# Per-batch quantiser shifts, an earlier set-up of the second pass, and a verdict by a matrix product in a four-block attention kernel

## The chip, the cores and the metric

The kernel runs on one core of a Trainium2 chip. The core has a matrix engine (TensorE, PE), a vector engine (VectorE, DVE), an engine for elementwise functions (ScalarE, ACT), a general engine (GpSimd, POOL) and an engine that only issues transfers (SyncE, SP). Each works through its own instructions in the order in which the program was built, and waits on semaphores for the others. Transfers (DMAs) are issued from SP and from POOL and run beside them. The metric is the device time of one execution in microseconds (us), the median of several.

## The reference

Four attention blocks work one after the other on `x` (4 batches, 1024 tokens, 288 channels, 16 heads of 18). Blocks 0 and 3 have quantised linear layers, block 1 is a plain attention with a second set of keys. The change lies in block 2, whose attention quantises its inputs and its probabilities with one step for the whole tensor, cut from the reference:

```
def _fake_quant(x, n_bits, always_zero=False):
    levels = float(2 ** n_bits - 1)
    if always_zero:
        delta = stop_gradient(jnp.max(x) / levels); zp = 0.0
    ...
    xq = jnp.clip(_ste_round(x / delta) + zp, 0.0, levels)
    return (xq - zp) * delta

q, k, v = (_fake_quant(t, 8) for t in (q, k, v))
probs = jax.nn.softmax(einsum('bhqd,bhkd->bhqk', q, k) * scale, axis=-1)
probs = _fake_quant(probs, 8, always_zero=True)
out = einsum('bhqk,bhkd->bqhd', probs, v).reshape(b, s, 288) @ Wo + bo
...
h = h + _quant_attention(ln(h), ln(h), Wq1, ...)      # over 1024 tokens
h = h + _quant_attention(ln(h), context, Wq2, ...)    # over 64 context tokens
h = h + (a * gelu(gate)) @ Wff2 + bff2                # a, gate = ln(h) @ Wff1 + bff1
```

The step of the probabilities is the largest probability of the whole tensor, divided by 255. So no probability can be rounded before every row's sum and maximum are known.

## The kernel before

The kernel keeps `x` in on-chip memory and runs blocks 0 to 3. It counts on input ranges in which its short forms hold: the helper `watch_range` (L1213) writes for each watched tensor whether it left its range into a column of `bad`. At the end `verdict` (L1197) joins the columns, and if any is set the program runs a general path instead of keeping its result. A branch on the loaded value stands on every engine.

Block 2 has three stages.

*Stage 1* makes the queries, keys and values and writes them to a scratch area in main memory, with their global minima and maxima.

*`fq_passes`* (L2812) is the attention over 1024 tokens. Pass 1 reads queries, keys and values back (`in<-raw`, issued on SP), rounds them to levels, transposes them on PE, and ACT copies them into `qk` (all batches' queries and keys, head by head). The helper `operands` does a tile's transposes and copy; those of batch b+1 are placed among the scores of batch b. Then, for each batch, group of heads, 128 queries and pair of heads, PE makes scores (L3244), ACT takes two exponentials with row sums (L2891) into a buffer `e`, of which there are four (pool `f1e`), and DVE takes the row maxima `top` (L2898): 256 such steps.

Between the passes `prob_shift` (L2365) computes for each row and head the number that, added to the row's scores, makes the exponential come out directly as a quantiser level: reciprocal of the sums (L2373), range watch, product with `top`, maximum over all (`prob_params`, L820: on DVE, then on POOL by `partition_all_reduce`), then `log_shift` (L830) with a logarithm on ACT (L837) corrected by one exponential (L840), and the result split into three bf16 parts (L2383). All of this works on one 128x512 array, which is 32 tiles of 16 heads. ACT loads a function table between Ln and Exp. `add_shift` (L2389) puts a tile's three parts beside the 18 channels of each head: POOL copies them into `spad` (L2393), PE transposes (L2399), DVE adds to `qk` (L2400). Queries of a group of heads are multiplied with `kz`, a copy of the keys spread over zeros; `kz` is zeroed once by POOL and filled by DMAs on SP (`spread`, L2999; four transfers a turn, two tiles `kz0` and `kz1` in turn).

Pass 2 (`attend_levels`, L3253) makes the scores again (L3284), exponentials (L3293), rounding on DVE (L3296) and products with the values. The shifts of later tiles, the output projection and the next queries are made beside it.

*`fq_tail`* is the attention over 64 context tokens and the feed-forward part. It too calls `prob_shift`, with `top` and `sums` in the pool `f2q`. Behind it SP loads the feed-forward weights (L2408, L113) into memory that this pool has given back, then a bias (L3117) and, for each half batch, the queries (`qT<-qb`, L3127). POOL's copies into `spad` and the rest of `add_shift` follow for each tile.

What sets the order: the framework collects the program, assigns each instruction to its engine and lists them there by a scheduler that moves instructions by the time at which it thinks them ready. So the text's order and an engine's order can differ. Memory comes from pools on a stack: what a new pool takes from one that was closed must wait until the last user of the old one has finished. That wait stands on the engine that first writes the new memory. In the kernel before, the pool `f1o` (with `g2`, `b2`, `bo2`, `wq2`, `spad`, `kz`) is opened after the pool of `top` and `sums` was closed.

Of the kernel before, what the change touches and what calls it, by code (L numbers as in the profile page):

```python
# [18 lines left out]

# [2 lines left out]

# [6 lines left out]
F32 = mybir.dt.float32  # L29
BF16 = mybir.dt.bfloat16  # L30
I32 = mybir.dt.int32
AF = mybir.ActivationFunctionType
ALU = mybir.AluOpType
# [3 lines left out]
P = 128  # L37
B, S, C, H, D, T, FF = 4, 1024, 288, 16, 18, 64, 1152
NTB = S // P
NT = B * NTB  # L40
CK, NC3 = 96, 3
HP = 32
NG = 4
# [1135 lines left out]
class Fast(Net):  # L1179
# [16 lines left out]
    def verdict(self):  # L1196

        nc = self.nc
        s = self.cp.tile([P, 1], F32, name="bads")
        nc.vector.tensor_reduce(s, self.bad, AX.X, ALU.max)  # L1200
        al = self.cp.tile([P, 1], F32, name="bada")
        nc.gpsimd.partition_all_reduce(al, s, P, bass_isa.ReduceOp.max)
        fl = self.cp.tile([1, 1], mybir.dt.int32, name="badi")
        nc.vector.tensor_copy(fl, al[0:1, :])
        return nc.values_load(fl[0:1, 0:1])

    @contextmanager
# [1157 lines left out]
    def prob_shift(self, gp, tp, top, sums, step):  # L2365


        nc = self.nc
        flat = lambda ap: ap.rearrange("p t h -> p (t h)")
        rstep = gp.tile([P, 1], F32, name="rstep")  # L2370
        nc.vector.reciprocal(rstep, step)
        r = tp.tile([P, NT * H], F32, name="rs")
        nc.vector.reciprocal(r, flat(sums))  # L2373
        self.watch_range(self.R_MIN, self.R_MAX, r, "wr")
        u = flat(top)
        nc.vector.tensor_tensor(r, r, u, ALU.mult)
        pd = self.prob_params(gp, r, "pd")
        nc.vector.memset(u, 0.0)
        self.log_shift(tp, u, flat(sums), pd, "ls")
        nc.vector.tensor_scalar(u, u, rstep, None, ALU.mult)  # L2380
        parts = gp.tile([P, 3, NT * H], BF16, name="parts")
        for k in range(3):
            nc.vector.tensor_copy(parts[:, k, :], u)  # L2383
            if k < 2:
                nc.vector.tensor_tensor(u, u, parts[:, k, :], ALU.subtract)
        return pd, parts

    def add_shift(self, qT, sp, parts, t):


        nc = self.nc
        for k in range(3):
            nc.gpsimd.tensor_copy(  # L2393
                sp[:, :, D + k : D + k + 1], parts[:, k, t * H : (t + 1) * H].unsqueeze(2)
            )
        ps = self.ps1(BF16)
        sf = sp.rearrange("p h d -> p (h d)")
        for g in range(NG):
            nc.tensor.transpose(ps[:, g * P : (g + 1) * P], sf[:, g * P : (g + 1) * P], self.idb)  # L2399
        nc.vector.tensor_tensor(  # L2400
            qT, qT, ps[:, : NG * P].rearrange("p (g t) -> p g t", t=P), ALU.add
        )
# [410 lines left out]
    def fq_passes(self, w, q, step, raw, rawq, qmx, qmn, side, aside):  # L2813

        tc, nc = self.tc, self.nc
        with ExitStack() as es:
            pool = lambda name, bufs, **k: es.enter_context(tc.tile_pool(name=name, bufs=bufs, **k))
            gp = pool("f1h", 1)
            wo = gp.tile([P, NG, C], F32, name="wo")
            nc.sync.dma_start(wo, w["Wo1p"].rearrange("(g p) o -> p g o", p=P))  # L2820
            rstep = self.scale_register("lstep", step)
            qk = gp.tile([P, B, 2, NG, S], BF16, name="qk")
            v = gp.tile([P, NT, C + HP - D], BF16, name="v")
            nc.gpsimd.memset(v[:, :, C:], 0.0)

            tops = ExitStack()
            tp = tops.enter_context(tc.tile_pool(name="f1m", bufs=1))
            top = tp.tile([P, NT, H], F32, name="top")
            sums = tp.tile([P, NT, H], F32, name="sums")
            with (  # L2830
                tc.tile_pool(name="f1l", bufs=3) as ld,
                tc.tile_pool(name="f1a", bufs=1) as at,
                tc.tile_pool(name="f1e", bufs=4) as ep,
                tc.tile_pool(name="f1x", bufs=3, space=PSUM) as self.pa,
                tc.tile_pool(name="f1y", bufs=2, space=PSUM) as self.pb,
            ):
# [22 lines left out]
                def operands(b, j):  # L2859

                    ps = self.ps1(BF16)
                    pf = pads[(b * NTB + j) % 4].rearrange("p n h d -> p (n h d)")
                    for m in range(2 * NG):
                        nc.tensor.transpose(
                            ps[:, m * P : (m + 1) * P], pf[:, m * P : (m + 1) * P], self.idb
                        )
                    nc.scalar.copy(
                        qk[:, b, :, :, j * P : (j + 1) * P].rearrange("p n g t -> p (n g) t"),
                        ps.rearrange("p (m t) -> p m t", t=P),
                    )  # L2870
# [3 lines left out]
                for b in range(B):  # L2874
                    ahead = levels(b + 1) if b + 1 < B else None
                    for g in range(NG):
                        for qt in range(NTB):
                            t = b * NTB + qt

                            n = g * NTB + qt  # L2880
# [17 lines left out]
                                nc.vector.tensor_reduce(top[:, t, h0 : h0 + 2], e, AX.X, ALU.max)  # L2898
                    if ahead:
                        operands(b + 1, NTB - 1)  # L2900
            with tops:
                pd, parts = self.prob_shift(gp, tp, top, sums, step)
            es.enter_context(self.psum("f1o"))

            pv = gp.tile([P, 1], F32, name="pv")
            nc.vector.tensor_tensor(pv, pd, q["d"][:, 2:3], ALU.mult)
            nc.vector.tensor_scalar(wo, wo, pv, None, ALU.mult)
            at, ot, ep = pool("f1o", 1), pool("f1q", 2), pool("f1p", 2)
            g2 = self.load_bc(at, w["ln2_g"], C, "g2")
            b2 = self.load_bc(at, w["ln2_b"], C, "b2")  # L2910
            bo2 = self.load_bc(at, w["bo2"], C, "bo2")
            wq2 = self.load_w(at, w["Wq2"], C, "wq2")
            spad = at.tile([P, H, HP], BF16, name="spad")
            nc.gpsimd.memset(spad, 0.0)

            def shifts(b, hf):
                for j in range(hf * 4, hf * 4 + 4):
                    t = b * NTB + j
                    self.add_shift(qk[:, b, 0, :, j * P : (j + 1) * P], spad, parts, t)
                    yield  # L2920

            def output(t0, oT):

                yield
                yield
                for j in range(4):
                    ps = self.ps1()
                    for k in range(NG):
                        nc.tensor.matmul(
                            ps[:, :C],  # L2930
                            lhsT=oT[:, k, j * P : (j + 1) * P],
                            rhs=wo[:, k, :],
                            start=(k == 0),
                            stop=(k == NG - 1),
                        )
                        if k == 1:
                            yield
                    xt = self.x[:, t0 + j, :]
                    nc.vector.tensor_tensor(xt, xt, ps[:, :C], ALU.add)
                    yield  # L2940
# [45 lines left out]
                        nc.sync.dma_start(rawq[t // NTB][:, t % NTB, :], y)  # L2986
                        yield

            kzs = [at.tile([P, 2, S], BF16, name=f"kz{n}") for n in range(2)]
            for kz in kzs:  # L2990
                nc.gpsimd.memset(kz, 0.0)

            def spread(n):

                kz = kzs[n % 2]
                b, g = n // (2 * NG), n % NG
                for i in range(4):
                    rows = slice(i * HP, (i + 1) * HP)
                    nc.sync.dma_start(kz[rows, i % 2, :], qk[rows, b, 1, g, :])  # L2999

            spread(0)
            side.append(shifts(0, 0))
            while side:
                aside()
            late = []
            for b in range(B):
                for qh in range(2):
# [18 lines left out]
    def fq_tail(self, w, kq, keep, rawq, mx, nmn, beside):  # L3026
# [4 lines left out]
        tc, nc = self.tc, self.nc  # L3031
        with ExitStack() as es:
            pool = lambda name, bufs, **k: es.enter_context(tc.tile_pool(name=name, bufs=bufs, **k))
            gp, dr = pool("f2g", 1), pool("f2d", 1, space=bass.MemoryType.DRAM)
            wo = gp.tile([P, NG, C], F32, name="wo")
# [3 lines left out]
            with (  # L3039
# [7 lines left out]
                top = qp.tile([P, NT, H], F32, name="top")  # L3047
                sums = qp.tile([P, NT, H], F32, name="sums")
# [6 lines left out]
                q = self.global_params(gp, mx, nmn, "qq")  # L3055
                self.watch_range(-0.5, 255.5, q["zp"], "qzext")
                step = gp.tile([P, 1], F32, name="step")
# [3 lines left out]
                rstep = self.scale_register("cstep", step)  # L3061

                for t in range(NT):
                    b, j = divmod(t, NTB)
                    pd = pads[t % 3]
# [4 lines left out]
                    ps = self.ps1(BF16)  # L3070
# [9 lines left out]
                    for m in range(2):  # L3080
                        ps = self.ps1()
                        for g in (2 * m, 2 * m + 1):
                            nc.tensor.matmul(
                                ps[:, (g % 2) * 256 : (g % 2 + 1) * 256],
                                lhsT=qT[:, g, :],
                                rhs=kt["kbd4"][:, b, g, :],
                                start=True,
                                stop=True,
# [10 lines left out]
                    e4 = self.wk.tile([P, H, T // 4], F32, tag="e4", name="e4")  # L3099
                    nc.gpsimd.tensor_tensor(e4, e2[:, :, : T // 4], e2[:, :, T // 4 :], ALU.add)  # L3100
                    nc.vector.tensor_reduce(sums[:, t, :], e4, AX.X, ALU.add)
                pd, parts = self.prob_shift(gp, qp, top, sums, step)
            pv = gp.tile([P, 1], F32, name="pv")
            nc.vector.tensor_tensor(pv, pd, kq["d"][:, 1:2], ALU.mult)
            nc.vector.tensor_scalar(wo, wo, pv, None, ALU.mult)
# [302 lines left out]
```

## Time and profile before

| | |
|---|---|
| median of 3 runs | 5169.89 us (5169.68 to 5172.34) |
| the profiled execution, its own time | 5169.41 us |
| its span | 5167.7 us |
| mean granted PE clock | 0.836 |
| busy: PE, ACT, DVE, POOL | 4402.1 (85%), 3131.3 (61%), 2961.2 (57%), 1395.9 (27%) us |
| block 2, pass 1, about | 1854 to 2456 us |
| between the passes, last maximum to first exponential of pass 2 | 2455.84 to 2484.47 us |
| tail: last sum to first exponential after `prob_shift` | 3182.56 to 3220.10 us |
| last `y` done, last residual adds begun, end | 5151.90, 5160.35, 5167.7 us |

The span runs from the first to the last recorded instruction of one execution; the time of that execution is 1.7 us longer. In the views, a group's line has the engine, the operation, the tile written and those read, the shape, then the busy time, the mean duration in ns, and behind the second bar the idle time ahead of it with what ended most of it. A line of the timeline has the start, the duration (of a row of like instructions together, with their number behind x), the engine, and in brackets the idle time before it. "SPq" is an issue of a transfer on SP.

### The profile page before, as it was taken

How to read it: one execution, taken by the hardware profiler on the slowest of the kernel's cores; microseconds unless marked ns; L12 is line 12 of the kernel's file. 1: busy time of each engine (PE TensorE's matmuls, PEld its weight loads, DVE VectorE, ACT ScalarE, POOL GpSimd, SP SyncE). 2: the span in 40 equal slices, each digit the busy share in tenths (PEclk: the TensorE clock that was granted, in tenths of full speed). 3: DMA queues.
4: the chain of work that ended last, by engine and by line, in shares of the span. 5: the costliest groups of instructions: out<-in, count | busy, mean ns of one | idle time of the engine just before them, and what ended most of it. 6: DMA issues, size and time to landing. Idle time of an engine off the chain costs nothing. (4 is left out here: it accounts for less than half of the span.)

```text
span 5167.7 us, 63518 instructions
## 1 busy us (share of the span) xinstructions
PE 4402.1 (85%) x23067; PEld 1767.0 (34%) x23067; DVE 2961.2 (57%) x6478; ACT 3131.3 (61%) x4422; POOL 1395.9 (27%) x2173
## 2 busy tenths in 40 slices
PE   5999997788899979998688863899988999996786
PEld 2223222445566521100232332454542222222343
DVE  8333243665564569999687877432334334334775
ACT  2767665466653259999788853212215766674796
POOL 4020111442421457300122234111113021103664
PEclk8999998889999965555687875899997999997897
DMA  2000002200001221000000032000000000001000
GB/s 74 4 5 12 3 21 54 68 25 15 2 12 40 101 87 35 14 1 0 23 24 24 23 98 79 20 15 10 1 15 1 8 4 9 18 21 31 16 17 20
DMA packets 135541, 135.64 MB, mean 26 GB/s; under 512 B 69260, under 2 KB 111884, under 8 KB 133552
## 3 DMA queue, kind: packets, MB, share of 16 engines
q1 hardware_dynamic: 134016, 127.79, 8.2%
q0 software_dynamic: 1200, 3.69, 0.3%
q8 instruction: 183, 3.00, 0.2%
q14 instruction: 142, 1.16, 0.1%
HBM read 79.59 MB, written 43.47 MB: 24 GB/s over the span
## 5 line engine op out<-in xcount | busy, mean ns | idle before, releaser
L2004 ACT ACTIVATE e<-ps 128x1024 f32<-128x1024 f32 x1024 | 998.9, 1021 | 481.9 <-PE ps L1994 471.3
L1994 PE MATMUL ps<-qT,kT 32*128 32x512 f32 x4096 | 704.4, 662 | 5.2 <-ACT e L2004 5.2
L1954 PE MATMUL ps<-e,v 128*32 128x512 f32 x4096 | 573.6, 625 | 11.4 <-DVE oT L1965 9.1
L2898 DVE TENSOR_REDUCE top<-e 128x2 f32<-128x2048 f32 x256 | 561.9, 2322 | 18.6 <-ACT e L2891 18.6
L2891 ACT ACTIVATE e<-ps 128x1024 f32<-128x1024 f32 x512 | 534.0, 1369 | 19.6 <-PE ps L3244 11.3
L3293 ACT ACTIVATE e<-ps 128x1024 f32<-128x1024 f32 x512 | 484.2, 1056 | 89.7 <-PE ps L3284 71.4
L3244 PE MATMUL ps<-qk 32*128 32x512 bf16 x1024 | 511.1, 604 | 24.3 <-ACT e L2891 23.0
L1747 POOL TENSOR_TENSOR x<-x,y 128x288 f32<-128x288 f32 x192 | 152.0, 803 | 826.3 <-DVE y L1746 758.7
L1404 POOL TENSOR_TENSOR h<-h,g 128x288 f32<-128x288 f32 x224 | 181.5, 813 | 645.5 <-ACT h L1401 606.7
L3296 DVE TENSOR_SCALAR eb<-e 128x2048 bf16<-128x2048 f32 x256 | 321.9, 1261 | 49.3 <-ACT e L3293 47.0
L1994 PEld LDWEIGHTS ps<-qT,kT 32*128 32x128 f32 x4096 | 204.9, 189 | 227.4 <-issue 143.3
L2891 ACT ACTIVATION_READ_ACCUMULATOR e<-ps 128x1 f32 x512 | 280.6, 550 | 0.0
L3284 PE MATMUL ps<-qk,kz 64*128 64x512 bf16 x1024 | 228.9, 445 | 43.0 <-ACT e L3293 39.9
L2437 PE MATMUL psf<-hT,w 128*128 128x512 f32 x576 | 257.9, 600 | 0.6 <-ACT hT L2429 0.6
L1954 PEld LDWEIGHTS ps<-e,v 128*32 128x32 f32 x4096 | 83.0, 109 | 424.4 <-issue 349.5
L1349 PE MATMUL ps<-idb,q 128*128 128x128 bf16 (+2 forms) x1152 | 114.6, 245 | 119.8 <-ACT q L1333 67.7
L1401 ACT ACTIVATE h<-x,nmr,rstd 128x288 f32<-128x288 f32 x224 | 130.2, 622 | 139.2 <-DVE nmr L1393 68.1
L3244 PEld LDWEIGHTS <-qk 32*128 32x128 bf16 x1024 | 52.8, 99 | 465.1 <-issue 465.1
L3193 ACT ACTIVATE gl<-psf,bf 128x512 f32<-128x512 f32 x72 | 46.0, 684 | 270.6 <-PE psf L2441 266.0
L1354 ACT COPY qT<-ps 98x384 bf16<-98x384 bf16 (+3 forms) x256 | 151.6, 641 | 72.6 <-PE ps L1349 72.4
L277 PEld LDWEIGHTS <-qT 98*128 98x128 bf16 (+2 forms) x1344 | 136.1, 105 | 129.9 <-issue 45.5
L1405 POOL TENSOR_TENSOR h<-h,b 128x288 f32<-128x288 f32 x224 | 179.9, 806 | 0.3
(483 smaller groups left out, 7725.3 us busy)
## 6 DMA issues: line engine op xcount, KB each, us to landing
raw<-y SPq DMA_DIRECT2D x32, 432.0 KB
in<-raw SPq DMA_DIRECT2D x32, 432.0 KB
kz<-qk SPq DMA_DIRECT2D x128, 64.0 KB
wn<-in_L_wfc SPq DMA_DIRECT2D x12, 432.0 KB
x<-in_x SPq DMA_DIRECT2D x4, 1152.0 KB
vvo<-vt SPq DMA_DIRECT2D x16, 288.0 KB
vo<-vvo SPq DMA_DIRECT2D x4, 1152.0 KB
rawq<-y SPq DMA_DIRECT2D x32, 144.0 KB
```

The costliest lines, as they stand in the source:

```text
L1404: nc.gpsimd.tensor_tensor(h, h, g, ALU.mult)
L1405: nc.gpsimd.tensor_tensor(h, h, beta, ALU.add)
L1954: nc.tensor.matmul(acc[i * HP : (i + 1) * HP, :], lhsT=st["v"][:, kt, h * (D + 1) : h * (D + 1) + HP], rhs=es_[i // 2][:, i % 2, :], start ...
L1994: nc.tensor.matmul(pss[i // 2][:, i % 2, :], lhsT=self.row_tile(kT, i)[:, kt * P : (kt + 1) * P], rhs=self.row_tile(qT, i)[:, qh * 512 : ( ...
L2004: nc.scalar.activation(e, ps, AF.Exp, scale=SCALE)
L2437: nc.tensor.matmul(o, lhsT=lhs(i)[:, c, :], rhs=rhs(i)[:, c, :], start=(c == 0), stop=False)
L2891: nc.scalar.activation(e[:, j, :].rearrange("p (a n) -> p a n", a=2), sc, AF.Exp, scale=rstep, accum_out=sums[:, t, h0 + j : h0 + j + 1],)
L2898: nc.vector.tensor_reduce(top[:, t, h0 : h0 + 2], e, AX.X, ALU.max)
L3244: self.nc.tensor.matmul(ps[:, c, :], lhsT=self.row_tile(qT, i)[:, g, qt * P : (qt + 1) * P], rhs=self.row_tile(kT, i)[:, g, c * 512 : (c + ...
L3284: nc.tensor.matmul(pss[i][:, n, :], lhsT=kz[rows, i, kt * P : (kt + 1) * P], rhs=qT[rows, g, qh * 512 : (qh + 1) * 512], start=True, stop= ...
L3293: nc.scalar.activation(e[:, 2 * n : 2 * n + 2, :], ps, AF.Exp, scale=step)
L3296: nc.vector.tensor_scalar(eb, e, MAGIC, MAGIC, ALU.add, ALU.subtract)
```

## The change

The change has four parts.

1. `verdict` joins the 128 partitions by a product with a column of ones on PE, in one bank of a new pool, and DVE copies the 1x1 result to an integer. The `partition_all_reduce` on POOL is no longer made.
2. `prob_shift` returns, beside the global step, one function for each batch. Each makes the shift of its 128x128 quarter, with its own tiles `y`, `z` and `parts`. The reciprocal, the product with `top` and the global maximum are still made on the whole. The product goes into `top`, and the range watch moves behind the last batch's shift.
3. `fq_passes` opens the pool `f1o` before the pool of `top` and `sums`, so that the loads, the zeros of `spad` and `kz` and the first keys don't need the memory of `top`. The first `spread` is written right after pass 1. Then come batch 0's shift, its first four tiles, the other batches' shifts, and the scaling of `wo`. The pool of `e` has three buffers instead of four.
4. `fq_tail` calls the four functions one after the other.

```diff
     def verdict(self):
...
-        al = self.cp.tile([P, 1], F32, name="bada")
-        nc.gpsimd.partition_all_reduce(al, s, P, bass_isa.ReduceOp.max)
         fl = self.cp.tile([1, 1], mybir.dt.int32, name="badi")
-        nc.vector.tensor_copy(fl, al[0:1, :])
+        with self.psum8("bad"):
+            ps = self.ps1()
+            nc.tensor.matmul(ps[0:1, 0:1], lhsT=s, rhs=self.ones[:, 0:1], start=True, stop=True)
+            nc.vector.tensor_copy(fl, ps[0:1, 0:1])
         return nc.values_load(fl[0:1, 0:1])
...
     def prob_shift(self, gp, tp, top, sums, step):
...
         nc.vector.reciprocal(r, flat(sums))
-        self.watch_range(self.R_MIN, self.R_MAX, r, "wr")
-        u = flat(top)
-        nc.vector.tensor_tensor(r, r, u, ALU.mult)
-        pd = self.prob_params(gp, r, "pd")
-        nc.vector.memset(u, 0.0)
-        self.log_shift(tp, u, flat(sums), pd, "ls")
-        nc.vector.tensor_scalar(u, u, rstep, None, ALU.mult)
-        parts = gp.tile([P, 3, NT * H], BF16, name="parts")
-        for k in range(3):
-            nc.vector.tensor_copy(parts[:, k, :], u)
-            if k < 2:
-                nc.vector.tensor_tensor(u, u, parts[:, k, :], ALU.subtract)
-        return pd, parts
+        nc.vector.tensor_tensor(flat(top), r, flat(top), ALU.mult)
+        pd = self.prob_params(gp, flat(top), "pd")
+        parts = [gp.tile([P, 3, NTB * H], BF16, name=f"parts{b}") for b in range(B)]
+
+        def shift(b):
+            u = flat(top[:, b * NTB : (b + 1) * NTB, :])
+            nc.vector.memset(u, 0.0)
+            self.log_shift(tp, u, flat(sums[:, b * NTB : (b + 1) * NTB, :]), pd, f"ls{b}")
+            nc.vector.tensor_scalar(u, u, rstep, None, ALU.mult)
+            for k in range(3):
+                nc.vector.tensor_copy(parts[b][:, k, :], u)
+                if k < 2:
+                    nc.vector.tensor_tensor(u, u, parts[b][:, k, :], ALU.subtract)
+            if b == B - 1:
+                self.watch_range(self.R_MIN, self.R_MAX, r, "wr")
+
+        return pd, parts, [partial(shift, b) for b in range(B)]
...
     def add_shift(self, qT, sp, parts, t):
...
-                sp[:, :, D + k : D + k + 1], parts[:, k, t * H : (t + 1) * H].unsqueeze(2)
+                sp[:, :, D + k : D + k + 1],
+                parts[t // NTB][:, k, t % NTB * H : (t % NTB + 1) * H].unsqueeze(2),
...
     def fq_passes(self, w, q, step, raw, rawq, qmx, qmn, side, aside):
...
+            at = pool("f1o", 1)
+            g2 = self.load_bc(at, w["ln2_g"], C, "g2")
+            b2 = self.load_bc(at, w["ln2_b"], C, "b2")
+            bo2 = self.load_bc(at, w["bo2"], C, "bo2")
+            wq2 = self.load_w(at, w["Wq2"], C, "wq2")
+            spad = at.tile([P, H, HP], BF16, name="spad")
+            nc.gpsimd.memset(spad, 0.0)
+            kzs = [at.tile([P, 2, S], BF16, name=f"kz{n}") for n in range(2)]
+            for kz in kzs:
+                nc.gpsimd.memset(kz, 0.0)
+
+            def spread(n):
...
             tops = ExitStack()
...
-                tc.tile_pool(name="f1e", bufs=4) as ep,
+                tc.tile_pool(name="f1e", bufs=3) as ep,
...
-            with tops:
-                pd, parts = self.prob_shift(gp, tp, top, sums, step)
+            spread(0)
+            pd, parts, shift = self.prob_shift(gp, tp, top, sums, step)
             es.enter_context(self.psum("f1o"))
-
-            pv = gp.tile([P, 1], F32, name="pv")
-            nc.vector.tensor_tensor(pv, pd, q["d"][:, 2:3], ALU.mult)
-            nc.vector.tensor_scalar(wo, wo, pv, None, ALU.mult)
-            at, ot, ep = pool("f1o", 1), pool("f1q", 2), pool("f1p", 2)
-            g2 = self.load_bc(at, w["ln2_g"], C, "g2")
...
+            shift[0]()
+            for _ in shifts(0, 0):
+                pass
+            for f in shift[1:]:
+                f()
+            tops.close()
+
+            pv = gp.tile([P, 1], F32, name="pv")
+            nc.vector.tensor_tensor(pv, pd, q["d"][:, 2:3], ALU.mult)
+            nc.vector.tensor_scalar(wo, wo, pv, None, ALU.mult)
+            ot, ep = pool("f1q", 2), pool("f1p", 2)
...
-            kzs = [at.tile([P, 2, S], BF16, name=f"kz{n}") for n in range(2)]
-            for kz in kzs:
-                nc.gpsimd.memset(kz, 0.0)
...
-            spread(0)
-            side.append(shifts(0, 0))
-            while side:
-                aside()
...
     def fq_tail(self, w, kq, keep, rawq, mx, nmn, beside):
...
-                pd, parts = self.prob_shift(gp, qp, top, sums, step)
+                pd, parts, shift = self.prob_shift(gp, qp, top, sums, step)
+                for f in shift:
+                    f()
```

More of the change, by code (lines that the diff above doesn't have):

```diff
@@ L21 @@
 from contextlib import ExitStack, contextmanager
+from functools import partial
 import concourse.bass as bass
@@ L2824, in fq_passes @@
             nc.gpsimd.memset(v[:, :, C:], 0.0)
+            at = pool("f1o", 1)
[9 more added lines that the diff above has]
+            def spread(n):
+                kz = kzs[n % 2]
+                b, g = n // (2 * NG), n % NG
+                for i in range(4):
+                    rows = slice(i * HP, (i + 1) * HP)
+                    nc.sync.dma_start(kz[rows, i % 2, :], qk[rows, b, 1, g, :])
             tops = ExitStack()
@@ L2900, in fq_passes @@
                         operands(b + 1, NTB - 1)
-            with tops:
-                pd, parts = self.prob_shift(gp, tp, top, sums, step)
+            spread(0)
+            pd, parts, shift = self.prob_shift(gp, tp, top, sums, step)
             es.enter_context(self.psum("f1o"))
-            pv = gp.tile([P, 1], F32, name="pv")
-            nc.vector.tensor_tensor(pv, pd, q["d"][:, 2:3], ALU.mult)
-            nc.vector.tensor_scalar(wo, wo, pv, None, ALU.mult)
-            at, ot, ep = pool("f1o", 1), pool("f1q", 2), pool("f1p", 2)
-            g2 = self.load_bc(at, w["ln2_g"], C, "g2")
[L2910 to L2914, printed above, removed]
             def shifts(b, hf):
@@ L2987, in queries @@
                         yield
-            kzs = [at.tile([P, 2, S], BF16, name=f"kz{n}") for n in range(2)]
-            for kz in kzs:
[L2991 to L2999, printed above, removed]
-            spread(0)
-            side.append(shifts(0, 0))
-            while side:
-                aside()
             late = []
```

## The prediction

> **What bounds the kernel now.** I read the page's chain and costliest groups first, then the timeline in four windows: the end, pass 1 of block 2, the hand-over from pass 1 to pass 2, and the start of the tail. The chain that ended last names only the end of the program, so it can't price a change in the middle. The groups give the rate of pass 1.
>
> ```profile
> issue 0%; POOL 0%
> ...
> L2898 DVE TENSOR_REDUCE top<-e 128x2 f32<-128x2048 f32 x256 | 561.9, 2322 | 18.6 <-ACT e L2891 18.6
> L2891 ACT ACTIVATE e<-ps 128x1024 f32<-128x1024 f32 x512 | 534.0, 1369 | 19.6 <-PE ps L3244 11.3
> ```
>
> Pass 1 (1854 to 2456 us) is held by VectorE (DVE): 256 reductions of 2.32 us, with 18.6 us idle in all. ScalarE (ACT) makes one `e` in about 2.0 us against 2.19 us from one reduction's start to the next, so it runs ahead until the buffers of `e` are full.
>
> The hand-over, in the timeline (start, duration, engine, line; in brackets the idle time before and its releaser):
>
> ```profile
> 2455.67 3.43 DVE L2373 RECIPROCAL rs<-sums 128x512 f32<-128x512 f32 x1
> ...
> 2470.60 0.43 DVE L2383 CAST parts<-top 128x512 bf16<-128x512 f32 x1
> ...
> 2471.63 0.74 POOL L107 DMA_DIRECT2D g<-in_L_ln_g  x1 [9.19 <-DVE parts L2383]
> ...
> 2473.90 3.58 POOL L2991 MEMSET kz<- 128x2048 bf16 x2
> ...
> 2477.40 0.54 POOL L2393 COPY spad<-parts 128x16 bf16<-128x16 bf16 x3
> ...
> 2484.47 1.94 ACT L3293 ACTIVATE e<-ps 128x1024 f32<-128x1024 f32 x2 [18.71 <-PE ps L3284]
> ```
>
> One chain: reciprocal, maximum, GpSimd (POOL) all-reduce (2462.07), Ln (2463.19), table load (1.28), Exp (2465.13), ten DVE steps to 2471.03; then POOL's loads and memsets to 2477.48, because the memory they fill is that of `top` and `rs`; then 1.33 us a tile for the shifts, and at 2484.47 the first exponential of pass 2. All engines are in this chain, so a microsecond saved is a microsecond of time.
>
> The tail has the same chain, but its last step releases a queue:
>
> ```profile
> 3197.74 0.49 DVE L2383 CAST parts<-top 128x512 bf16<-128x512 f32 x1
> ...
> 3198.39 0.39 SPq L2408 DMA_DIRECT2D w<-in_L_Wff  x1
> ...
> 3199.35 10.29 SPq L3117 DMA_DIRECT2D bf<-in_L_bff  x1
> ...
> 3217.80 1.52 DVE L2400 TENSOR_TENSOR qT<-qT,ps 128x512 bf16<-128x512 bf16 x4 [19.56 <-DMA qT<-qb]
> ```
>
> SP's weight load needs memory in which `top` stood, so it goes 0.16 us after the last cast; behind it on SP stand the bias load (10.29 us of issue) and the loads of `qT`. DVE is idle 19.56 us for `qT`, ACT 27.27 us. Whatever delays the last cast delays the stage one for one.
>
> The end:
>
> ```profile
> 5151.38 0.52 DVE L1746 SCALAR_TENSOR_TENSOR y<-ps,sc,wfc2sw 128x288 f32<-128x288 f32 x1 [2.61 <-PE ps L277]
> 5152.62 0.38 POOL L1202 PARTITION_ALL_REDUCE bada<-bads  x1 [5.87 <-DVE y L1746]
> 5153.03 0.14 DVE L1204 CAST badi<-bada 1x1 int32<-1x1 f32 x1 [1.13 <-POOL bada L1202]
> 5160.35 1.53 POOL L1747 TENSOR_TENSOR x<-x,y 128x288 f32<-128x288 f32 x2 [7.36 <-issue]
> ```
>
> The all-reduce comes late and, worse, the last two residual adds stand behind it on POOL, 7.36 us with no releaser ("issue"). I read this as POOL changing its program for the all-reduce and back: the trace has records of a new POOL configuration at 5146.9, before it, and at 5152.95, after it. Everything after 5160.35 waits for them.
>
> **What the Trainium skill says.** "ScalarE: Activation LUTs", What ACT_TABLE_LOAD costs: a load is about 1283 ns plus a drain of about 1380 ns. The trace has the load, 1.28 us, but not the drain: Ln ends at 2463.82, Exp starts at 2465.13. Its section on table sets says that one set holds both exp and ln; the trace disagrees for this program, a load stands between them. "VectorE: DVE Perf Modes", on the fixed latency per instruction: an fp32 tensor_tensor takes (N+151)/0.96 ns. For 512 that is 0.69 us, as the trace shows; for 128 it is 0.29 (my estimate from the page), so a quarter of the data costs over 40% of the time. On POOL's program change I found no price; the trace gives 5.87 and 7.36 us.
>
> **The change part by part.**
>
> *Loads, zeros and keys set up ahead.* Three POOL loads, 0.56 us memset, 3.58 us of memsets and one SP load now stand ahead of stage 1's own. POOL idles 44.98 us until 1655.08 (its next load waits for DVE's `bad` of block 1); about 6 us go into this hole, cost nothing. Without that cover they would add 6. The eight key copies (5.04 us of SP issue) go into pass 1 among SP's loads, whose users are many microseconds behind: nothing.
>
> *Three buffers for `e` instead of four.* The program's order also moves the `qk` copies forward: 268 exponentials before the last, instead of 290. An `e` with a copy costs ACT 0.89 us more. Before, DVE's distance behind ACT shrinks through that stretch to 1.04 us at its least, and then grows to 4.3. With three buffers it can hold about one reduction, 2.2 us, and copies now come closer together. Following both engines with those rates I get 0 to 1.9 us of extra idle time on DVE: +1.0. Bounds for the unknown: 0 and +3.
>
> *Shift by batch, hand-over.* One DVE maximum (0.6) leaves the way ahead of the all-reduce (the other still stands there), and other small steps go: all-reduce 0.9 earlier, 2461.15. `Ln` of batch 0 follows at about 2462.1. At 128x128 I take ACT 0.31 (between 0.21 at 128x8 and 0.63 at 128x512), DVE 0.29 for two operands and 0.21 to 0.23 for one, start to start 0.08 less where nothing depends. But ACT's order is now Ln0, Ln1, load, Exp0, load, Ln2, load, Exp1, Exp2, load, Ln3, load, Exp3: six loads instead of two (+4 × 1.28 = 5.1). DVE's in-order stream takes batch 1's product before batch 0's first parts, so three loads stand ahead: Exp1 ends at 2462.1 + 4 × 0.31 + 3 × 1.28 + 0.2 = about 2467.4. Some 14 DVE steps of 0.18: parts of batch 0 at 2469.9 (whole tensor before: 2471.03). POOL's copies then start at once, 0.3 to 0.4 us later the first transpose, 2470.3 against 2477.98. The tiles' cadence stays, so the first exponential comes at 2484.47 − 7.7 = 2476.8; DVE's remaining casts and the scaling of `wo` (0.82) hold back the first `eb` by some 0.2. Gain 7.5, bounds 6 and 8.5. It consists of 6.4 us of POOL work that left the way and 1.1 us of earlier parts.
>
> *Shift by batch, tail.* All four batches are made before anything else, so here the loads and small steps count in full. The maximum comes 0.65 earlier (3188.9). Parts of batch 0 at about 3197.2; batch 3's last DVE product before its Ln stands behind these, so Ln3 3198.1, load, Exp3 to about 3199.9, then some 20 DVE steps of 0.2 (among them `wo`, 0.81): last cast over at 3203.8, against 3198.23. Cost +5.6, bounds +4.5 and +7.5. SP's queue starts by that much later, and `qT` with it.
>
> *Verdict by a product.* No program change: the adds stand directly after the last `y` (5151.90), the output leaves at 5152.8 instead of 5161.9. The product of 128x1 with ones is a matmul of the smallest size, about 0.1; the cast comes with the last `y`, at 5152.0 instead of 5153.03. What is then last is the branch: before, cast to the engines being past the branch took 3.8 us or so (the registers' loads at 5153.2, PE's branch over near 5157). So 5152.15 + 0.5 + 3.6 = 5156.3; POOL's closing instructions (0.70, drain 2.11, semaphores) 3.25, and 0.8 to the span's end, as before: 5160.4 against 5167.7. Gain 7.3, bounds 6.2 and 9.1 (if only the adds had been late).
>
> Sum: −7.5 + 1.0 + 5.6 − 7.3 = −8.2. The profiled execution took 5169.4 us (span 5167.7), so 5161.2; the median of the runs shown lies 0.5 above it: about 5161.6.
>
> **Rivals.** About 0.2%, 10.3 us, is what a measurement of this kernel can tell from no change: below 5159.5 is faster, above 5180.2 slower.
>
> 1. *The tail pays less, the end gives all.* If Ln3 does not stand behind batch 0's casts, the tail costs the two extra pairs of loads alone, 2 to 3 us, and the end 9.1: −7.5 + 0.5 + 2.5 − 9.1 = −13.6, 5156.3. For it: POOL's 7.36 idle us are beyond doubt. Against: in the changed program's order on DVE, which is fixed when it is built, it does. 0.31.
> 2. *The loads and small steps cost the hand-over too.* If batch 0's parts come at 2472 instead of 2469.9, the gain there is 5.4; the tail +7.5, the end −6.2, pass 1 +1.5: −2.6, 5167.3. For it: 128x128 steps are interpolated. 0.19.
> 3. *Pass 1 becomes coupled, slower.* With three buffers ACT may wait for each release, so that each `e` costs DVE a handshake. 0.1 us over 256 is 25.6 us: −8.2 − 1.0 + 25.6 = +16.4, 5186. It decides from 0.075 us per `e` (18.5 us in all). Against: ACT needs 2.0 of each 2.19 us, so one buffer ready suffices. 0.15.
> 4. *Nothing happens.* If the swap or POOL's loads only moved to another place on the chain, within 3 us of 5169.9. Both have vanished or gone into a hole of 45 us. 0.03.
>
> **How the numbers follow.** The likeliest case, 0.32, has 5161.6, own range 5159.5 to 5164. Rivals 1 and 2 reach 5154.5 and 5170; a weak form of 3 (0.04 us per `e`) goes a little beyond: 5154.5 to 5174 leaves out the outer part of 1 and most of 3. Faster: rival 1 and the lowest of the likeliest, 0.35. Slower: rival 3, 0.15. Same: the rest, 0.50.
>
> **What would show it.** In the hand-over: POOL's first `spad` copy near 2470 with no load or memset before it; first exponential near 2477.8 (pass 1's +1 included); six table loads. In the tail: SP's weight load some 5.6 us later against the reciprocal of `sums`. At the end: no all-reduce, adds directly after `y`, from last `y` to the span's end 8.5 us instead of 15.8. In pass 1: DVE idle near 19.6 us, not 18.6. The prediction is wrong if DVE's idle time in pass 1 grows by over 5, or if the branch costs more when it is nothing's cover.

## The result, and the profile after

The changed kernel takes 5186.23 us (median of 6 runs, 5179.55 to 5195.91), the kernel before in the same comparison 5169.78 us (6 runs, 5166.31 to 5174.2). The ratio is 1.0031 with a 95% interval of 1.0021 to 1.0041, or 11 to 21 us more. It is slower, and by more than the 10.3 us within which the prediction would have seen no difference. The forecast was 5161.6 us, with no such difference as the likeliest outcome. Single runs of one kernel scatter by 10 to 25 us, so the steps below are compared inside the profiles, where most stages repeat to 0.1 us (the end to 0.4).

The profiled execution took 5191.71 us, its span is 5189.9 us. Its stages against those of before, in us:

| from, to | before | after | measured | predicted |
|---|---|---|---|---|
| pass 1: first maximum to reciprocal | 572.11 | 595.05 | +22.9 | +1.0 |
| hand-over: reciprocal to first exponential of pass 2 | 28.80 | 21.39 | −7.4 | −7.5 |
| tail: reciprocal to SP's weight load | 15.63 | 21.15 | +5.5 | +5.6 |
| end: last `y` done to the span's end | 15.79 | 8.52 | −7.3 | −7.3 |
| sum | | | +13.7 | −8.2 |

The two spans differ by 22.2 us. Of the 8.5 us that the table leaves, 8.8 lie ahead of block 2's global maxima (1853.11 against 1861.88), in work whose instructions and order on DVE, ACT and PE did not change; the other stages add −0.3. Of these 8.8, 8.5 are there when DVE comes to the step that starts at 997.0 us before and at 1005.5 after, and the first of the loads that were moved forward is issued at 1617.44, so these loads are not the cause. I take them for the scatter of single runs. The medians are 16.5 us apart.

Pass 1 first. The costliest groups of the kernel after (busy time and mean, then the idle time ahead of it and its releaser):

```profile
L2927 DVE TENSOR_REDUCE top<-e 128x2 f32<-128x2048 f32 x256 | 564.2, 2277 | 39.1 <-ACT e L2920 38.4
...
L2920 ACT ACTIVATE e<-ps 128x1024 f32<-128x1024 f32 x512 | 522.4, 1108 | 41.4 <-PE ps L3260 31.7
```

The maxima are as long as before, but DVE is idle for 39.1 us instead of 18.6, waiting for ACT. ACT is idle 41.4 instead of 19.6, waiting for PE. So it is PE that is late. PE's transposes in pass 1, in the groups of that stretch, before:

```profile
L2864 PE MATMUL ps<-idb,pads 128*128 128x128 bf16 x204 | 27.1, 309 | 18.1 <-POOL pads L2856 16.5 <-ACT qk L2867 1.1 <-DVE pads L2856 0.5
```

and after:

```profile
L2893 PE MATMUL ps<-idb,pads 128*128 128x128 bf16 x208 | 29.9, 307 | 47.4 <-POOL pads L2885 44.8 <-ACT qk L2896 2.1 <-DVE pads L2885 0.5
```

PE stands 44.8 us ahead of its transposes until POOL has made their `pads`, instead of 16.5. One such stop in the timeline after:

```profile
2019.63 1.97 POOL L2885 TENSOR_SCALAR pads<-in,gqtop 128x288 bf16<-128x288 f32 x2
...
2020.69 0.61 PE L2893 MATMUL ps<-idb,pads 128*128 128x128 bf16 x4 [3.96 <-POOL pads L2885]
...
2021.63 0.32 SPq L2878 DMA_DIRECT2D in<-raw  x1
...
2023.27 1.02 ACT L2920 ACTIVATE e<-ps 128x1024 f32<-128x1024 f32 x1 [3.68 <-PE ps L3260]
...
2024.41 4.48 DVE L2927 TENSOR_REDUCE top<-e 128x2 f32<-128x2048 f32 x2 [3.51 <-ACT e L2920]
...
2025.16 0.98 POOL L818 TENSOR_SCALAR in<-in,gqrd 128x288 f32<-128x288 f32 x2 [3.56 <-DMA in<-raw]
```

PE works in order: the scores behind the waiting transposes wait too, then ACT (3.68 us), then DVE (3.51 us). The last line shows why POOL is slow: the next load is issued at 2021.63, the moment POOL has done the `pads` that held the buffer, and POOL waits 3.56 us for it.

The later tiles are the 24 of batches 1 to 3, numbered 0 to 23. From the eighth of them on, POOL makes the pads of a tile only after it has rounded the tile after next; so its three load buffers are all in use, and the load stands in line with POOL's work. POOL's time from tile to tile there is 12.0 us (11.7 in the kernel before), with about 8.2 of work in it. PE's order asks for a tile each 9.9 us. What lies between these rates was covered by PE's asking late. In the trace before, the copy of the second of these tiles comes after 40 exponentials and the last after 244; in the changed kernel after 22 and 222. From the third tile on, each copy stands 20 or 22 exponentials earlier. Since two banks of PSUM (the memory into which PE writes) let PE run two tiles ahead of the copies, PE wants tile 21 right after the copy of tile 19. Before, that copy came after 208 exponentials and started 233.7 us after the first maximum, and the pads of tile 21 were done at 232.7. The reserve, counted to the copy's start, was 1.0 us. In the changed kernel the copy comes after 186: 22 exponentials at 1.1 us are 24.1 us, which makes the reserve −23.1. Three intervals between maxima at the start of the pass are over 2.3 us in both traces; the changed kernel has 25 more, and what these have beyond 2.19 us adds up to 22.7 us.

The hand-over after, in the timeline:

```profile
2487.59 3.34 DVE L2377 RECIPROCAL rs<-sums 128x512 f32<-128x512 f32 x1
...
2494.45 1.28 ACT L841 ACT_TABLE_LOAD   x1
...
2496.07 1.28 ACT L838 ACT_TABLE_LOAD   x1
...
2497.70 1.28 ACT L841 ACT_TABLE_LOAD   x1
...
2500.27 0.22 DVE L2388 CAST parts<-top 128x128 bf16<-128x128 f32 x1
...
2500.56 0.25 POOL L2401 COPY spad<-parts 128x16 bf16<-128x16 bf16 x1 [7.20 <-DVE parts L2388]
...
2508.98 7.44 ACT L3309 ACTIVATE e<-ps 128x1024 f32<-128x1024 f32 x8 [3.69 <-POOL spad L2401]
```

Three table loads, then batch 0's first part, then POOL's copy at once, with no loads or memsets ahead of it. From the reciprocal to PE's first transposes it is 14.6 us (2502.21), as predicted (2470.3 against 2455.67).

The tail after:

```profile
3205.13 3.35 DVE L2377 RECIPROCAL rs<-sums 128x512 f32<-128x512 f32 x1
...
3220.46 0.31 ACT L838 ACTIVATE ls3z<-ls3y 128x128 f32<-128x128 f32 x1 [2.05 <-DVE ls3y L836]
...
3225.92 0.22 DVE L2388 CAST parts<-top 128x128 bf16<-128x128 f32 x1
...
3226.29 0.38 SPq L2417 DMA_DIRECT2D w<-in_L_Wff  x1
...
3245.53 1.52 DVE L2409 TENSOR_TENSOR qT<-qT,ps 128x512 bf16<-128x512 bf16 x4 [18.70 <-DMA qT<-qb]
```

Batch 3's Ln stands behind the parts of batches 0 and 1. Its last cast ends 21.0 us after the reciprocal, SP's load goes at once, and `qT` follows. The end after:

```profile
5180.87 0.52 DVE L1748 SCALAR_TENSOR_TENSOR y<-ps,sc,wfc2sw 128x288 f32<-128x288 f32 x1 [2.61 <-PE ps L278]
...
5181.44 0.19 PE L1205 MATMUL ps<-ones,bads 128*1 128x1 f32 x2 [0.68 <-DVE y L1748]
5181.47 0.79 POOL L1749 TENSOR_TENSOR x<-x,y 128x288 f32<-128x288 f32 x1 [2.34 <-DVE y L1748]
5181.74 0.14 DVE L1206 CAST badi<-ps 1x1 int32<-1x1 f32 x1 [0.35 <-PE ps L1205]
```

The residual add starts 0.08 us after `y`, where it waited 7.36 us before.

### The profile page after: what moved, and what is told of

It is laid out like the page before. It is cut to its first block, busy times and chain, and to the rows that moved or that the text cites. A ratio compares the mean times of both kernels' runs of the same rounds, so it can differ in the third digit from the quotient of the medians.

```text
span 5189.9 us, 63602 instructions
## 1 busy us (share of the span) xinstructions
PE 4384.2 (84%) x23069; PEld 1766.0 (34%) x23069; DVE 2965.6 (57%) x6550; ACT 3145.9 (61%) x4442; POOL 1394.4 (27%) x2172
## 5 line engine op out<-in xcount | busy, mean ns | idle before, releaser
L2927 DVE TENSOR_REDUCE top<-e 128x2 f32<-128x2048 f32 x256 | 564.2, 2277 | 39.1 <-ACT e L2920 38.4
L1956 PE MATMUL ps<-e,v 128*32 128x512 f32 x4096 | 573.7, 625 | 11.7 <-DVE oT L1967 9.1
L2920 ACT ACTIVATE e<-ps 128x1024 f32<-128x1024 f32 x512 | 522.4, 1108 | 41.4 <-PE ps L3260 31.7
L3260 PE MATMUL ps<-qk 32*128 32x512 bf16 x1024 | 489.9, 605 | 39.4 <-ACT e L2920 38.2
L3213 DVE SCALAR_TENSOR_TENSOR u<-psf,bf,gl 128x512 f32<-128x512 f32 x72 | 51.3, 747 | 213.2 <-ACT gl L3209 213.2
```

Source lines behind the costliest of these rows:

```text
L1956: nc.tensor.matmul(acc[i * HP : (i + 1) * HP, :], lhsT=st["v"][:, kt, h * (D + 1) : h * (D + 1) + HP], rhs=es_[i // 2][:, i % 2, :], start ...
L2920: nc.scalar.activation(e[:, j, :].rearrange("p (a n) -> p a n", a=2), sc, AF.Exp, scale=rstep, accum_out=sums[:, t, h0 + j : h0 + j + 1],)
L3260: self.nc.tensor.matmul(ps[:, c, :], lhsT=self.row_tile(qT, i)[:, g, qt * P : (qt + 1) * P], rhs=self.row_tile(kT, i)[:, g, c * 512 : (c + ...
```

## The experiments

The theory (A): with three buffers of `e` the program's order takes the transposes some 20 exponentials forward, and PE then stands waiting for POOL's pads. Its rivals: (B) the keys, zeros and loads that were brought forward into pass 1's queues cost the time; (C) the added time is not pass 1's at all; and, within pass 1, (D) the buffers cost it by themselves, since ACT can run less far ahead of DVE.

**Three buffers alone** in the kernel before:

```diff
-                tc.tile_pool(name="f1e", bufs=4) as ep,
+                tc.tile_pool(name="f1e", bufs=3) as ep,
```

> The kernel before with one edit: three buffers of e in pass 1 instead of four. Theory A (the three buffers let the program's order put the transposes of the next batch's tiles some 20 exponentials earlier; PE then reaches them before POOL has made their pads and stands still, and ACT and DVE behind it): the whole loss of pass 1 shows here, 19 to 24 us, so about 5192 us, with DVE idle near 39 us in pass 1 and PE waiting for POOL. Rival B (the early keys, zeros and loads in pass 1's queues cost it, not the buffers): 5169 to 5172. Rival C (the added time is spread over the whole program by the chip's clock and not in pass 1): about 5170.

Measured: 5195.19 us against 5173.53, ratio 1.0048 (1.0035 to 1.0061). Pass 1 takes 595.48 us, with DVE idle as in the changed kernel:

```profile
L2898 DVE TENSOR_REDUCE top<-e 128x2 f32<-128x2048 f32 x256 | 564.2, 2277 | 39.5 <-ACT e L2891 38.8
...
L2864 PE MATMUL ps<-idb,pads 128*128 128x128 bf16 x208 | 30.0, 308 | 47.7 <-POOL pads L2856 42.2 <-ACT e L2891 2.9 <-ACT qk L2867 2.1
```

One number in the code gives the whole loss. B and C fall: nothing was brought forward here, and the stage is as long as in the changed kernel within 0.5 us.

**Four buffers again** in the changed kernel. The memory doesn't hold them beside everything that was set up early, so one of the two zeroed key tiles and the query weights move behind the shifts:

```diff
-            wq2 = self.load_w(at, w["Wq2"], C, "wq2")
...
-            kzs = [at.tile([P, 2, S], BF16, name=f"kz{n}") for n in range(2)]
-            for kz in kzs:
-                nc.gpsimd.memset(kz, 0.0)
+            kzs = [at.tile([P, 2, S], BF16, name="kz0")]
+            nc.gpsimd.memset(kzs[0], 0.0)
...
-                tc.tile_pool(name="f1e", bufs=3) as ep,
+                tc.tile_pool(name="f1e", bufs=4) as ep,
...
+            at = pool("f1r", 1)
+            wq2 = self.load_w(at, w["Wq2"], C, "wq2")
+            kzs.append(at.tile([P, 2, S], BF16, name="kz1"))
+            nc.gpsimd.memset(kzs[1], 0.0)
```

> The changed kernel with four buffers of e again; for the room, the second zeroed key tile and the second query weights are set up behind the shifts, and only the first ahead of pass 1. Theory A: the copies stand where they stood in the kernel before, pass 1 gives back 19 to 24 us, everything else keeps: about 5162 to 5165 (the sum of hand-over -7.5, tail +5.5, end -7.3 against 5169.9). Rival B: no better than 5180.

Measured: 5165.49 us, ratio to the kernel before 0.9986 (0.9978 to 0.9993). Pass 1 is back at 572.21 us, the hand-over keeps its 21.32. PE's transposes wait as in the kernel before:

```profile
L2891 PE MATMUL ps<-idb,pads 128*128 128x128 bf16 x208 | 27.8, 309 | 19.1 <-POOL pads L2883 16.5 <-ACT qk L2894 2.1 <-DVE pads L2883 0.5
```

The time off the kernel before, 8.0 us (3.6 to 11.4), agrees with the predicted sum without its term for pass 1 (−7.5 + 5.6 − 7.3 = −9.2).

**One bank for the transposes**, with three buffers in the kernel before. PE can then be only one tile ahead of the copies:

```diff
-                tc.tile_pool(name="f1e", bufs=4) as ep,
+                tc.tile_pool(name="f1e", bufs=3) as ep,
...
-                tc.tile_pool(name="f1y", bufs=2, space=PSUM) as self.pb,
+                tc.tile_pool(name="f1y", bufs=1, space=PSUM) as self.pb,
```

> The kernel before with three buffers of e, and one bank instead of two for the transposes. If PE's standing still is the time by which POOL's pads are late, one bank less lets PE meet each tile one copy later: 20 exponentials later in all, 19.9 us, while POOL's order puts pads behind the loads two tiles earlier, 6.6 us against it. So 13 of the 23 us vanish: pass 1 (first maximum to reciprocal) 580 to 585 us, against 595.5 with two banks. If the buffers themselves, through the distance of ACT ahead of DVE, cost the time, pass 1 stays at 595.

Of this kernel and the next one execution each was taken (5176.92 and 5179.6 us), so only their stages are compared. Measured: 585.98 us from the first maximum, just outside the expected range. But one of the copies ahead of the first maximum has moved behind it, and the first maximum comes 4.6 us sooner after the global maxima of the inputs (25.88 against 30.47). With it each later copy stands 8 to 10 exponentials further back; so this edit delays both the copies and PE's asking. Measured from there to the reciprocal, 625.95 us with two banks become 611.86: 14.1 us vanish, where 13 were expected. PE's wait for pads:

```profile
L2864 PE MATMUL ps<-idb,pads 128*128 128x128 bf16 x216 | 30.6, 308 | 34.5 <-POOL pads L2856 31.0 <-ACT qk L2867 3.3 <-DVE pads L2856 0.2
```

31.0 instead of 42.2 us, where the kernel before has 16.5. The buffers of `e` are the same three, and yet 14.1 us are gone: D can't say that.

**A tile's load in three pieces**, with three buffers in the kernel before, so that POOL can begin with the first:

```diff
-                        nc.sync.dma_start(y, raw[b][:, j, :])
+                        for n in range(3):
+                            cols = slice(n * C, (n + 1) * C)
+                            nc.sync.dma_start(y[:, cols], raw[b][:, j, cols])
```

> The kernel before with three buffers of e, and each tile of queries, keys and values loaded by three transfers instead of one. If the loss follows POOL's pace of 11.7 us a tile, of which 3.4 us are its wait for the load, a first third that lands about 1.3 us earlier takes that off each tile: pass 1 577 to 588 us instead of 595.5, and POOL's time from tile to tile about 10.4 us. If POOL's pace is no cause, pass 1 stays at 595.

Measured: pass 1 takes 581.58 us, 13.9 less. POOL's pace over tiles 9 to 20 goes from 12.0 to 11.1 us, 0.9 instead of the 1.3 expected, and its wait for the loads is 34.4 us:

```profile
L817 POOL TENSOR_SCALAR in<-in,gqrd 128x288 f32<-128x288 f32 x72 | 37.0, 515 | 53.1 <-DMA in<-raw 34.4 <-DVE in L817 18.7
```

(50.3 with three buffers and whole loads.) Both experiments leave the three buffers as they are and take off some 14 of the 23 us. What remains in each, 9 us, goes with pads that are still late (PE waits 31.0 and 27.9 us for POOL).

The traces also show stretches in which three buffers cost nothing. Behind the three long intervals at the start, the 40 intervals between maxima ahead of the first stop take 87.74 us with three buffers alone, with seven copies among them, and 87.73 in the kernel before. The 149 behind the last stop take 326.81 and 326.76. With the loads in three pieces the first stop comes later, and the 58 intervals ahead of it take 127.27 us, against 127.20 in the kernel before. So A stands. Within the stops, where a fourth buffer could let DVE work on for a little while PE waits, the part of D was not separated.

**The tail in one piece**, with the four buffers of the second experiment: `prob_shift` of the kernel before is kept under a second name and called in `fq_tail` alone.

```diff
-                pd, parts, shift = self.prob_shift(gp, qp, top, sums, step)
-                for f in shift:
-                    f()
+                pd, parts = self.prob_shift_whole(gp, qp, top, sums, step)
```

> As the last one, but the tail's shift made in one piece, as in the kernel before. If the tail's step is worth what its last cast came later (5.4 us), this takes 5.4 us less than the run with four buffers and the shift by batch in the tail: about 5157 to 5159. If the later release of SP's queue is hidden further on, the two are equal.

Measured: 5158.78 us, 0.9972 (0.9962 to 0.9981) of the kernel before, 6.7 us less than with the tail by batch (1.8 to 11.1 when the runs are resampled). The weight load goes 15.64 us after the reciprocal instead of 21.16, 5.5 us sooner. So the work behind doesn't hide this step.

**The hand-over alone**: the last kernel with the verdict of before.

```diff
+        al = self.cp.tile([P, 1], F32, name="bada")
+        nc.gpsimd.partition_all_reduce(al, s, P, bass_isa.ReduceOp.max)
         fl = self.cp.tile([1, 1], mybir.dt.int32, name="badi")
-        with self.psum8("bad"):
-            ps = self.ps1()
-            nc.tensor.matmul(ps[0:1, 0:1], lhsT=s, rhs=self.ones[:, 0:1], start=True, stop=True)
-            nc.vector.tensor_copy(fl, ps[0:1, 0:1])
+        nc.vector.tensor_copy(fl, al[0:1, :])
```

> The kernel before with the hand-over alone: early keys and zeros, shifts by batch between the passes, four buffers of e, the tail's shift in one piece and the verdict on POOL. By the step of the prediction 28.8 us from the reciprocal to the first exponential of pass 2 become 21.3, and the time falls by that: about 5162.3. Rival: pass 2 is bound by other work and gives it back, less than 3 us off the time.

Measured: 5160.64 us against 5172.82, 0.9981 (0.9974 to 0.9988). The hand-over takes 21.32 us instead of 28.69 to 28.80; 12.2 us by the medians are more than these 7.4, but the interval (6.2 to 13.4 us) holds them.

**The verdict alone** in the kernel before, which is the last diff the other way round:

> The kernel before with the new verdict alone. By the step of the prediction: from the end of the last y to the span's end 8.5 us instead of 15.8, the rest as before, so 7.3 us less, about 5162.5. If the branch's own time bounded the end before as well, the end is shorter by 3 us or less.

Measured: 5165.12 us, 0.9989 (0.998 to 0.9998), 7.7 us less by the medians. From the last `y` to the end it takes 8.47 us.

**Logarithm and exponential on the whole array** between the passes, in the kernel with four buffers and the tail in one piece:

```diff
+        ut, sf = flat(top), flat(sums)
+        nc.vector.memset(ut, 0.0)
+        yt = tp.tile([P, NT * H], F32, name="lsy")
+        nc.vector.tensor_scalar(yt, sf, pd, None, ALU.mult)
+        zt = tp.tile([P, NT * H], F32, name="lsz")
+        nc.scalar.activation(zt, yt, AF.Ln)
+        nc.vector.tensor_tensor(ut, ut, zt, ALU.subtract)
+        nc.scalar.activation(zt, zt, AF.Exp, scale=-1.0)
...
-            nc.vector.memset(u, 0.0)
-            self.log_shift(tp, u, flat(sums[:, b * NTB : (b + 1) * NTB, :]), pd, f"ls{b}")
+            w = slice(b * NTB * H, (b + 1) * NTB * H)
+            u, y, z = ut[:, w], yt[:, w], zt[:, w]
+            nc.vector.tensor_tensor(z, z, y, ALU.mult)
+            nc.vector.tensor_scalar(z, z, -1.0, 1.0, ALU.mult, ALU.add)
+            nc.vector.tensor_tensor(u, u, z, ALU.add)
```

> As the last one, and between the passes the logarithm and the exponential on the whole 128x512 array (two table loads instead of six), only the steps on DVE behind them by batch. If the four extra table loads hold back batch 0's parts, the first parts come 1.7 us earlier and the time is 1 to 2.5 us less, about 5156; if DVE's own steps hold them back, no difference.

In its timeline, one load stands between Ln and Exp:

```profile
2468.01 0.63 ACT L2387 ACTIVATE lsz<-lsy 128x512 f32<-128x512 f32 x1 [11.99 <-DVE lsy L2385]
...
2468.66 1.28 ACT L2389 ACT_TABLE_LOAD   x1
...
2469.95 0.63 ACT L2389 ACTIVATE lsz<-lsz 128x512 f32<-128x512 f32 x1
...
2472.38 0.38 POOL L2435 COPY spad<-parts 128x16 bf16<-128x16 bf16 x1 [5.41 <-DVE parts L2399]
```

The reciprocal begins at 2461.20, so POOL's first copy comes 11.2 us after it instead of 13.0, and the hand-over takes 19.67 us instead of 21.33: 1.7 us less, as expected. The median is 5155.65 us, 0.9969 (0.9956 to 0.9981) of the kernel before. The profile shows the gain over the kernel with the tail in one piece in the stage; the times, 5158.78 and 5155.65 with overlapping intervals, don't show it by themselves. This version is faster than both kernels of this study, by about 0.3% against the first.

## Why the prediction was wrong

Three of its four terms were right within 0.1 us, and each was shown alone. One failed.

*Three buffers for `e` instead of four*, the step forecast at +1.0, cost 22.9 us. It saw that the copies move forward and followed ACT's and DVE's rates through them, but not what a copy needs: transposes on PE, and for these the pads from POOL. The wait for these pads was put at nothing, without a reason; PE's wait for them grew from 16.5 to 44.8 us. I asked how often a copy costs ACT time, and not whether its tile would be there. (The step's own numbers were also put the wrong way: 268 and 290 are the exponentials that come after the last copy, in the kernel before and in the changed one.) The trace of before had the answer: POOL's pads for tile 21 were done 1.0 us before the copy behind which PE wants them. A move by 22 exponentials, 24.1 us, against a reserve of 1 us can't be free. The bounds of that step, 0 and +3, were those of the wrong model, and so the range ended at 5174. The prediction had named the sign of this failure itself, DVE's idle time in pass 1 growing by over 5 us; it grew by 20.5.

*The rival on the slower side* has almost the right time, 5186, but by luck, for its reason is wrong. It had a handshake of 0.1 us in each `e`. In the trace, the intervals between maxima are 2.19 us as before, but for the 25 stops where PE waits; the reserve of a whole engine ran out, not the one of a buffer. Its argument against itself, that one buffer ready suffices, is right as far as it goes. (Its limit is a slip: by its own sum it decides from 19.5 us, or 0.076 for each `e`.)

*Loads, zeros and keys ahead*: nothing, as said. The pass with three buffers and no early keys is as long as that of the changed kernel (595.48 and 595.05), and what the changed kernel had lost ahead of the pass was lost before these loads.

*Hand-over*: 7.4 for 7.5, and the order of ACT's loads was right. POOL's third copy, which needs batch 0's last part, starts 14.3 us after the reciprocal (2501.91); the step had the parts at 14.2 (2469.9). Its first copy comes 1.3 us sooner than that, since POOL takes each part when it is there. Rival 2, with the parts 2 us later, falls. (Between Exp and the last cast the trace before has nine steps on DVE, not ten; nothing rests on it.)

*Tail*: 5.5 for 5.6, by the mechanism named, Ln of batch 3 behind the parts of batches 0 and 1. Rival 1 had batch 3's Ln not behind the casts of batch 0, and 2 to 3 us. The timeline has it behind them, and the tail in one piece gives the time back. *Verdict*: 7.3 for 7.3; rival 1's full 9.1 doesn't come, since the engines' branches and POOL's closing drain then end last.

What the sum leaves open is small: +13.7 in the profile's stages, +16.5 between medians whose ratio holds 11 to 21.

## What to carry to other kernels

When a change moves an operation earlier in an engine's order, ask for each of its operands when the producer makes it, and how much reserve the trace shows; two engines that run at unlike rates (here 11.7 and 9.9 us a tile) may live on a head start that no line of the profile names. A buffer count is not only room: where a scheduler lays out the order with it, one buffer less moves instructions of other engines. And a step that is divided to give its first part early should be divided only where the first part is what is awaited: between the passes it was, in the tail the last part released the queue.

## What the runs showed of the hardware

The verdict's product of 128 values with ones is recorded as two matmuls of 0.19 us in all, and the cast behind it starts 0.35 us after DVE's last `y`; the same join on POOL stood between 5.87 us of waiting ahead of it and 7.36 us behind it.

ACT's busy time is no measure of its work: the same 512 exponentials have a mean of 1369 ns in the kernel before and 1108 in the slower one, and the reads of their accumulators 550 and 290. The long ones don't go with ACT's distance ahead of DVE. In the last 56 maxima of the kernel before, where ACT is 4.3 us ahead, the reads take 0.20 us, as in the changed kernel, where it is 2.2; between the 60th and the 106th maximum they take 1.01 us before, where ACT is 2.1 us ahead, and 0.25 in the changed kernel, where PE stands. What lengthens them was not tried.
